# The last two tiles of self-attention and the entry into the feed-forward: another order on TensorE, and PSUM waits by tile

## The chip, the cores and the metric

The kernel runs on one core of a Trainium2 chip. The metric is the device time of one execution in microseconds (us); a time without other words is the median of the runs. The core has five engines with queues of their own: TensorE (PE in the profile; its weight loads are PEld), VectorE (DVE), ScalarE (ACT), GpSimd (POOL) and SyncE (SP), which issues most of the DMAs. [...]

## What is computed

One layer over x of 32 sequences x 64 tokens x 512: a cross-attention to a memory of 1601 tokens per sequence, a causal self-attention with 16 heads of 32, and a feed-forward of 2048 hidden units, each added to x. All in fp32. Cut to what matters here:

```python
x = x + xattn(layernorm(x), ctx, mask, ...)          # stage 1
Q, K, V = heads(n @ WQ), heads(n @ WK), heads(n @ WV)  # stage 2, n = layernorm(x)
score = softmax(Q @ K.T / sqrt(32) + causal)
x = x + (score @ V) @ WO
h = gelu(x' @ absmean(W_fc).T)                        # stage 3, x' = layernorm(x)
h = (h - mean(h)) * rsqrt(var(h) + 1e-5) * ln_w + ln_b
x = x + h @ absmean(W_proj).T
```

absmean turns a weight matrix into -1, 0 and 1. The layer norm of h is applied behind the last product: the kernel needs for it the sums of h and of h squared over the 2048 units, and two rows of 512 numbers that depend on the weights alone, `ln_w @ W_proj` and `ln_b @ W_proj`. These two rows are the "sides".

## The kernel before, in words

The 2048 tokens lie in 16 tiles of 128, which stay in SBUF (`xres`, tile i is `xs[i]`). After the cross-attention comes `self_attention` (L1201), which works tile by tile (i from 0 to 15, loop at L1394), and then `feed_forward` (L1440), which works in 4 groups of 4 tiles. A group has 16 hidden units, and a unit is 128 of the 2048 hidden rows for 512 tokens. One unit is `hidden` (L1166): 8 matmuls into a PSUM tile `fh` (L1172; four with the high and four with the low half of the input, `fxh` and `fxl`), then on ScalarE gelu into `bank` (L1180) and a square `fsq` (L1182), and two additions on VectorE into `sums` (L1188, L1189), which the caller runs later through the function that `hidden` returns.

Tile i of the self-attention takes these steps:

- `normalise(i, s)`: VectorE divides the exponentials by their sum (`atot`, L1331 to L1333).
- `turn(i, s)`: PE transposes the scores in two PSUM tiles `aptp` (L1343); ScalarE and VectorE copy them into `wo` by turns, 8 copies, each waiting for the one before (L1348).
- `mix(i)`: 32 small matmuls into `po` (L1356), copied by ScalarE into `aoT` (L1364).
- `exponentials(i + 1)`: the scores of the next tile (`sc`, L1304), VectorE's scaling, maximum and subtraction (L1309 to L1319), and ScalarE's exponential (L1326).
- `self_out(i, oT)`: 8 matmuls from aoT into `aout` (L1370); VectorE adds the result to xres (L1373).

Between them, `next(steps)` puts in three chunks of other PE work per tile. Up to tile 13 these are the projections for the next pair of tiles (`aWQ`, `aWK`, `aV`). For the last two tiles there are no more, so `first_hidden` (L1281) gives the first 12 hidden units of the feed-forward instead, two to a chunk: units 0 to 5 in tile 14 and 6 to 11 in tile 15. `add_up` (L1288) runs the additions that are still due.

The sides are made at the end of tile 14 (`sides`, L1133): 16 matmuls into 4 rows of a PSUM tile (L1136) and a copy by VectorE (L1139). In tile 15, between `mix` and `self_out`, `spread` (L1141) brings the rows to all partitions: for each of two, a product (L1144, four matmul records in all) and a ScalarE copy (L1145).

The order of the work: `in_order` (L145) chains all PE, VectorE, ScalarE and GpSimd instructions of `self_attention` to the order in which the code issues them, engine by engine, and does the same for those of `feed_forward`. Between the two lists nothing is chained, so an instruction of the second list may come before a late one of the first on the same engine. The page and the timeline show this: hTh and hTl, the halves of the first units for the products y (`split`, L1505, with L1517 on ScalarE and L1518 on VectorE), run before the residual addition of tile 15.

PSUM has eight banks. In `self_attention` the tag "mm" has three of them in turn (all of aptp, aout, sides, spread, fh), the scores sc have four and po has one. In `feed_forward` the units have two (`fs_m`), the transposes and statistics two (`fs_t`) and the four outputs y of a group four (`fs_y`). A pool opens in the place of pools that were closed. As the kernel is written, the first tile of each new pool waits until everything that used the old pools in that place is done.

The feed-forward's first PE work is unit 12 into `fs_m`, then the products y (L1523) of unit 0 for four tiles, then on with a unit and 8 product matmuls by turns.

Of the kernel before, what the change touches and what calls it, by code (L numbers as in the profile page):

```python
# [26 lines left out]
PSUM = bass.MemoryType.PSUM  # L27
# [4 lines left out]
NT = B * T // P  # L32
# [7 lines left out]
GT = 4  # L40
# [40 lines left out]
def perceiver_kernel(ctx: ExitStack, tc: tile.TileContext, a: dict, out: bass.AP):  # L81
# [63 lines left out]
    def in_order(begin, kinds=(Engine.PE, Engine.DVE, Engine.Activation, Engine.Pool)):  # L145

        before = {}
        for ins in nc.cur_bb.bb.instructions[begin:]:
            if ins.engine not in kinds or isinstance(ins, mybir.BassTileRelease):
                continue  # L150
            if ins.engine in before:
                tc.add_manual_dep(
                    ins,
                    before[ins.engine],
                    mybir.DependencyInfo(mybir.DependencyClass.NoSync, mybir.DependencyReason.DATA),
                    reason="in order",
                )
            before[ins.engine] = ins.name
# [104 lines left out]
    with ExitStack() as st:  # L263
# [10 lines left out]
        m8, table, steps = (opening[:, i:j] for i, j in zip(CUTS, CUTS[1:]))  # L274
        table = table[:B].bitcast(F32).rearrange("p (k b) -> p k b", b=B)
        steps = steps[:B].bitcast(F32).rearrange("p (k c) -> p k c", c=NC)
# [793 lines left out]
    def load_piece(pool, j, why):  # L1070
        r = pool.tile([P, D], F32, tag="raw", name=f"raw_{why}_{j}")
        put = nc.sync.dma_start(r, pieces[j])
        if why == "g":
            tc.keep_in_program_order(put)
        return r
# [20 lines left out]
    def compare(pool, j, w):  # L1096

        r, k = load_piece(pool, j, "q"), j // FC
        nc.vector.tensor_scalar(w, r, thr[:, 1, k : k + 1], None, ALU.is_lt)
        nc.vector.scalar_tensor_tensor(  # L1100
            w, r, thr[:, 0, k : k + 1], w.bitcast(F32), ALU.is_gt, ALU.subtract
        )
# [98 lines left out]
    def self_attention(st, wf, wp, first, ffn_input, ffn_turned, hidden, sides, measured):  # L1201

        raw = st.enter_context(tc.tile_pool(name="raw", bufs=2))
        p1 = st.enter_context(tc.tile_pool(name="a1", bufs=1))
        p2 = st.enter_context(tc.tile_pool(name="a2", bufs=2))
        ps_m = st.enter_context(tc.tile_pool(name="as_m", bufs=3, space=PSUM))
# [13 lines left out]
        def piece_of(j):  # L1220
            return wf[:, j // 4, j % 4 * D : (j % 4 + 1) * D] if j < FC else wp[:, j - FC, :]

        def group_spreads(g):
            return spreads([xs[g * GA + t] for t in range(GA)], 1e-5, f"a{g}")
# [12 lines left out]
        def heads(g, xT, order=range(6)):  # L1237


            QT = p2.tile([P, DC, GA * P], F32, tag="QT", name=f"QT_{g}")  # L1240
            KT = p2.tile([P, DC, GA * P], F32, tag="KT", name=f"KT_{g}")
            V = p2.tile([P, GA, D], F32, tag="V", name=f"V_{g}")
            made[g] = QT, KT, V

            def turned(w, dst, m0, copy):
                ps = ps_m.tile([P, 2, GA * P], F32, tag="mm", name=f"a{w}_{g}_{m0}")
                for m in range(2):
                    for c in range(DC):
                        nc.tensor.matmul(  # L1249
                            ps[:, m, :],  # L1250
                            ws[w][:, c, (m0 + m) * P : (m0 + m + 1) * P],
                            xT[:, c, :],
                            start=(c == 0),
                            stop=(c == DC - 1),
                        )
                copy(dst[:, m0 : m0 + 2, :], ps)

            def values(i):
                ps = ps_m.tile([P, D], F32, tag="mm", name=f"aV_{g}_{i}")
                for c in range(DC):  # L1260
                    nc.tensor.matmul(  # L1261
                        ps,
                        xT[:, c, i * P : (i + 1) * P],
                        ws["WV"][:, c, :],
                        start=(c == 0),
                        stop=(c == DC - 1),
                    )
                nc.scalar.copy(V[:, i, :], ps)

            for k in order:  # L1270
                if k % 3 == 0:
                    turned("WQ", QT, 2 * (k // 3), nc.scalar.copy)
                elif k % 3 == 1:
                    turned("WK", KT, 2 * (k // 3), nc.vector.tensor_copy)
                else:
                    values(k // 3)
                yield
# [3 lines left out]
        def first_hidden():  # L1281

            for n in range(12):
                adds.append(hidden(n, first, ps_m, "mm", raw, "raw"))
                if n % 2:
                    yield

        def add_up():  # L1288
            for add in adds:
                add()  # L1290
            adds.clear()
# [32 lines left out]
        def exponentials(i):  # L1324
            s = scores(i)
            nc.scalar.activation(s, s, AF.Exp)  # L1326
            return s

        def normalise(i, s):
            tot = small.tile([P, HEADS], F32, tag="atot", name=f"atot_{i}")  # L1330
            nc.vector.tensor_reduce(tot, s, AX.X, ALU.add)  # L1331
            nc.vector.reciprocal(tot, tot)
            nc.vector.tensor_tensor(  # L1333
                s, s, tot.unsqueeze(2).to_broadcast([P, HEADS, T]), ALU.mult
            )

        def turn(i, s):
            pairs = s.rearrange("p (j e) k -> p j (e k)", e=2)
            into = pT.rearrange("p (j e) q -> p j e q", e=2)
            for j in range(0, HEADS // 2, 4):  # L1340
                tp = ps_m.tile([P, 4, P], F32, tag="mm", name=f"aptp_{i}_{j}")
                for k in range(4):
                    nc.tensor.transpose(tp[:, k, :], pairs[:, j + k, :], ident)  # L1343
                for b in range(2):
                    half = slice(b * T, (b + 1) * T)
                    for e in range(2):
                        eng = nc.vector.tensor_copy if e else nc.scalar.copy
                        eng(into[half, j : j + 4, e, half], tp[e * T : (e + 1) * T, :, half])  # L1348
# [18 lines left out]
        def self_out(i, oT):  # L1367
            ps = ps_m.tile([P, D], F32, tag="mm", name=f"aout_{i}")
            for c in range(DC):
                nc.tensor.matmul(  # L1370
                    ps, oT[:, c, :], ws["WO"][:, c, :], start=(c == 0), stop=(c == DC - 1)
                )
            nc.vector.tensor_tensor(xs[i], ps, xs[i], ALU.add)  # L1373
# [20 lines left out]
        for i in range(NT):  # L1394
            g, t = divmod(i, GA)
            ahead = g + 2 < groups
            k = (i - 5) // 2
            begun = list(chores.get(i, ()))
            if t == 0:
                steps = heads(g + 1, xT) if g + 1 < groups else first_hidden()  # L1400
            next(steps)
            normalise(i, s)
            add_up()
            next(steps)
            turn(i, s)
            add_up()
            if t == 0:
                if 5 < i < 13:
                    xns = apply(fsp)
                if ahead:  # L1410
                    sp = group_spreads(g + 2)
            else:
                if ahead:
                    axns = apply(sp)
                if 4 < i < 12:
                    fsp = spreads([xs[k]], 1e-5, f"f{k}")
            for j in begun[1:]:
                compare(raw, j, piece_of(j))
            next(steps)
            if t == 0:  # L1420
                if 5 < i < 13:
                    ffn_turned(k, xns[0], first, ps_m, "mm")
            elif ahead:
                xT = turned_group(g + 2, axns)
            oT = mix(i)
            if i + 1 < NT:
                s = exponentials(i + 1)
            else:
                spread()
            add_up()  # L1430
            self_out(i, oT)
            for j in begun[:1]:
                compare(raw, j, piece_of(j))
            if i == NT - 2:
                side = p1.tile([P, DC, GA * P], F32, tag="xT", name="side")
                spread = sides(ps_m, "mm", side.rearrange("p c t -> p (c t)")[:, :D])
        in_order(begin)
        return 12

    def feed_forward(st, wp, lnw, Wwb, sums, first, slot, ffn_input, ffn_turned, hidden, done, store):  # L1440
        fx = st.enter_context(tc.tile_pool(name="fx", bufs=1))
        ft = st.enter_context(tc.tile_pool(name="ft", bufs=3))
        fq = st.enter_context(tc.tile_pool(name="fq", bufs=2))
        ps_m = st.enter_context(tc.tile_pool(name="fs_m", bufs=2, space=PSUM))
        ps_t = st.enter_context(tc.tile_pool(name="fs_t", bufs=2, space=PSUM))
        ps_y = st.enter_context(tc.tile_pool(name="fs_y", bufs=GT, space=PSUM))
        second = [fx.tile([P, DC, GT * P], F32R, name=f"fx{k}_1") for k in ("h", "l")]
        inputs = [first, second]
        G = NT // GT
# [263 lines left out]
```

## Time and profile before

| what | value |
|---|---|
| runs | 904.86, 904.89, 901.55 us; median 904.86 |
| the profiled execution | 902.01 us, of which the span from first to last instruction is 899.1 |
| granted TensorE clock, mean | 0.998 |
| cross-attention and start, 0 to 500 us | TensorE busy 493.08 us |
| self-attention, 500 to 613 us | TensorE busy 113.00 of 113.00 us |
| last tiles, 613 to 642 us | TensorE busy 28.07 of 29.00 us |
| last tile and entry, 642 to 662.4 us | TensorE busy 18.98 of 20.40 us |
| feed-forward, 662.4 to 893 us | TensorE busy 230.21 of 230.60 us |

In the lines of the profile `aout<-bank,aoT` reads: writes aout, reads bank and aoT; "128*128 128x512 f32 x8" is the size of the weights, the shape of the moving operand, its type and how many. A bracket such as `[0.73 <-ACT aoT L1364]` gives the idle time of the engine just before the instruction and the instruction whose end ended it. Durations of neighbouring matmuls overlap, since they are pipelined: what a group takes from the engine is read from the start of one to the start of the next.

### The profile page before, as it was taken

Reading aid. Unit: us, or ns where it says so; the run is one execution under the profiler, and the core shown is the slowest. Engines: PE = TensorE matmul, PEld = TensorE weight load, DVE = VectorE, ACT = ScalarE, POOL = GpSimd, SP = SyncE. Lnnn points to the kernel's source line nnn. Section 1 sums busy time; section 2 is a strip of 40 time slices with the busy share of each in tenths; the row PEclk is TensorE's granted clock in tenths of the full one; section 3 lists DMA queues with packets and bytes.
Section 4 is the critical chain, followed back from the end, with each engine's and each line's share of the span. In section 5 each row is a group of like instructions: output and inputs, shape, how many; then the busy total and the mean of one; then the engine's idle time right before and its main releaser. Section 6 shows DMA issues by size and latency. Waiting matters only on the chain.

```text
span 899.1 us, 12923 instructions
## 1 busy us (share of the span) xinstructions
PE 883.5 (98%) x4536; PEld 635.2 (71%) x4536; DVE 626.6 (70%) x1198; ACT 377.9 (42%) x811; POOL 67.3 (7%) x79
## 2 busy tenths in 40 slices
PE   9999999999999999999999999999999999999997
PEld 4456777777777767667666776676668878788885
DVE  5875656455655672588889888886776886876864
ACT  2554545545445431222232323224555555555550
POOL 0110111111101100000000000000001000010000
PEclk9999999999999999999999999999999999999999
DMA  8975898775585343011111010100000020010101
GB/s 269 320 248 181 235 243 248 233 248 156 181 252 171 109 132 129 1 59 36 48 36 48 24 36 24 36 12 1 1 1 1 1 47 1 6 42 1 31 17 52
DMA packets 58723, 88.05 MB, mean 98 GB/s; under 512 B 10516, under 2 KB 30872, under 8 KB 58264
## 3 DMA queue, kind: packets, MB, share of 16 engines
q1 hardware_dynamic: 57888, 86.58, 32.0%
q8 instruction: 38, 0.62, 0.3%
q10 hardware_dynamic: 760, 0.55, 0.2%
q14 instruction: 37, 0.30, 0.1%
HBM read 78.72 MB, written 4.19 MB: 92 GB/s over the span
## 4 chain that ended last, share of the span: by engine, by line
PE 86%; DVE 9%; ACT 3%; issue 1%; DMA 1%; POOL 0%; POOLq 0%; ACTq 0%
PE y L1523 13%; PE kvp L523 13%; PE fh L1172 11%; PE xo L645 6%; PE aV L1261 5%; PE aWQ L1249 5%; PE aWK L1249 5%; PE aout L1370 5%; PE q L231 5%; PE lgp L565 3%; PE enc L629 3%; PE sc L1304 1%; PE pt L614 1%; PE aptp L1343 1%; PE po L1356 1%; DVE s L1309 1%
## 5 line engine op out<-in xcount | busy, mean ns | idle before, releaser
L523 PE MATMUL kvp<-wkv,ct 128*128 128x256 f32 x576 | 134.7, 379 | 0.0
L523 PEld LDWEIGHTS kvp<-wkv,ct 128*128 128x128 f32 x576 | 107.0, 190 | 21.6 <-issue 8.8
L1523 PE MATMUL y<-wp,hTh 128*128 128x512 f32 x236 | 94.4, 400 | 0.4 <-DVE xres L1500 0.4
L1523 PE MATMUL y<-wp,hTl 128*128 128x512 f32 x236 | 92.8, 393 | 0.0
L1172 PE MATMUL fh<-fxh,wf 128*128 128x512 f32 x256 | 71.6, 401 | 1.3 <-DVE mv_f L128 0.9
L1180 ACT ACTIVATE bank<-fh 128x512 f32<-128x512 f32 x64 | 38.2, 597 | 77.0 <-PE fh L1172 76.9
L1172 PE MATMUL fh<-fxl,wf 128*128 128x512 f32 x256 | 70.4, 397 | 0.0
L530 ACT ACTIVATE kv<-kvp,rstd 128x256 f32<-128x256 f32 x72 | 34.0, 473 | 82.4 <-PE kvp L523 82.3
L572 DVE CUSTOM_DVE_ANT_0 pr<-lgp,bias 128x384 f32<-128x384 f32 (+6 forms) x64 | 28.5, 458 | 50.6 <-PE lgp L565 50.3
L1370 PE MATMUL aout<-bank,aoT 128*128 128x512 f32 x128 | 59.2, 605 | 1.1 <-ACT aoT L1364 1.1
L1518 DVE SCALAR_TENSOR_TENSOR hTl<-bank,lnw,hTh 128x512 fp32r<-128x512 f32 x59 | 44.0, 749 | 20.7 <-ACT hTh L1517 20.7
L645 PE MATMUL xo<-wo,encT 128*128 128x512 f32 x128 | 57.7, 594 | 0.2 <-ACT encT L638 0.2
L231 PE MATMUL q<-xres,wo 128*128 128x512 f32 x128 | 56.4, 593 | 0.6 <-DVE wo L346 0.6
L1172 PEld LDWEIGHTS fh<-fxl,wf 128*128 128x128 f32 x256 | 48.3, 189 | 11.2
L1172 PEld LDWEIGHTS fh<-fxh,wf 128*128 128x128 f32 x256 | 46.6, 188 | 13.2 <-issue 2.2
L1523 PEld LDWEIGHTS y<-wp,hTh 128*128 128x128 f32 x236 | 44.4, 188 | 14.0 <-DVE xres L1500 3.4
L1188 DVE TENSOR_TENSOR sums<-sums,bank 128x512 f32<-128x512 f32 x56 | 38.5, 687 | 20.8 <-ACT bank L1180 20.7
L1326 ACT ACTIVATE s<-s 128x1024 f32<-128x1024 f32 x15 | 15.9, 1059 | 86.5 <-DVE s L1319 86.5
L1523 PEld LDWEIGHTS y<-wp,hTl 128*128 128x128 f32 x236 | 44.5, 188 | 9.9
L1261 PE MATMUL aV<-bank,axT 128*128 128x512 f32 x112 | 51.2, 600 | 0.0
L1348 ACT COPY wo<-aptp 64x256 f32<-64x256 f32 x64 | 23.3, 365 | 66.2 <-PE aptp L1343 48.9
L1249 PEld LDWEIGHTS aWQ<-axT,bank 128*128 128x128 f32 x224 | 42.6, 190 | 11.8 <-issue 6.7
(176 smaller groups left out, 1562.0 us busy)
## 6 DMA issues: line engine op xcount, KB each, us to landing
nat<-in_ctx_dram SPq DMA_DIRECT2D x64, 256.0 KB, 5.0
ct<-in_ctxT_dram SPq DMA_DIRECT2D x7, 768.0 KB, 4.6
xres<-in_x_dram SPq DMA_DIRECT2D x8, 512.0 KB, 6.3
xres<-in_x_dram SPq DMA_DIRECT2D x32, 128.0 KB, 5.1
qs<-bank SPq DMA_DIRECT2D x32, 128.0 KB, 3.8
raw_g<-in_W_fcT_dram SPq DMA_DIRECT2D x16, 256.0 KB, 4.5
raw_g<-in_W_projT_dram SPq DMA_DIRECT2D x16, 256.0 KB, 3.5
raw_q<-in_W_fcT_dram SPq DMA_DIRECT2D x16, 256.0 KB, 2.9
```

Source lines behind the costliest of these rows:

```text
L231: nc.tensor.matmul(ps, wq[:, c, h, :], wide(g)[:, c], start=(c == 0), stop=(c == DC - 1))
L523: nc.tensor.matmul(ps.rearrange("p k h -> p (k h)"), cts[p][:, c, j * P : (j + 1) * P], wkv[:, c].rearrange("p k h -> p (k h)"), start=(c ...
L530: nc.scalar.activation(kvs[p][:, j], ps, AF.Copy, scale=rstds[p][:, j : j + 1])
L645: nc.tensor.matmul(o, encT[:, h].rearrange("p s t -> p (s t)"), wo[:, h, :], start=(h == 0), stop=(h == NH - 1),)
L1172: nc.tensor.matmul(ps, wf[:, c, cols], part[:, c, :], start=(i == 0 and c == 0), stop=(i == 1 and c == DC - 1),)
L1180: nc.scalar.activation(g, ps, AF.Gelu)
L1188: nc.vector.tensor_tensor(sums[:, 0], so_far[0], g, ALU.add)
L1249: nc.tensor.matmul(ps[:, m, :], ws[w][:, c, (m0 + m) * P : (m0 + m + 1) * P], xT[:, c, :], start=(c == 0), stop=(c == DC - 1),)
L1261: nc.tensor.matmul(ps, xT[:, c, i * P : (i + 1) * P], ws["WV"][:, c, :], start=(c == 0), stop=(c == DC - 1),)
L1370: nc.tensor.matmul(ps, oT[:, c, :], ws["WO"][:, c, :], start=(c == 0), stop=(c == DC - 1))
L1518: nc.vector.scalar_tensor_tensor(lo, g, w, hi.bitcast(F32), ALU.mult, ALU.subtract)
L1523: nc.tensor.matmul(y, part[:, t, :], wp[:, c, :], start=(c == 0 and i == 0), stop=(c == FC - 1 and i == 1),)
```

## The change

Three edits, none of which adds or removes a matmul, a copy or a DMA.

- The sides are made in tile 14 between the scores of tile 15 and `self_out(14)`, where they came after `self_out(14)`.
- `first_hidden` yields after units 1, 3, 5, 7, 8, 10 and 11, where it yielded after every second one. In tile 15 the three chunks are now units 6 and 7, unit 8, units 9 and 10, and a fourth `next(steps)` puts unit 11 between `spread` and `self_out(15)`. A second `add_up` after `self_out` runs its additions; in all other tiles it finds none.
- The three PSUM pools of `feed_forward` get `reuse_waits="tile"`: a tile of the new pool waits for those old tiles alone that lay in its own place.

```diff
@@ first_hidden
             for n in range(12):
                 adds.append(hidden(n, first, ps_m, "mm", raw, "raw"))
-                if n % 2:
+                if n in (1, 3, 5, 7, 8, 10, 11):
                     yield
@@ the loop over the tiles
             else:
                 spread()
             add_up()
-            self_out(i, oT)
-            for j in begun[:1]:
-                compare(raw, j, piece_of(j))
             if i == NT - 2:
                 side = p1.tile([P, DC, GA * P], F32, tag="xT", name="side")
                 spread = sides(ps_m, "mm", side.rearrange("p c t -> p (c t)")[:, :D])
+            if i == NT - 1:
+                next(steps)
+            self_out(i, oT)
+            add_up()
+            for j in begun[:1]:
+                compare(raw, j, piece_of(j))
@@ feed_forward
-        ps_m = st.enter_context(tc.tile_pool(name="fs_m", bufs=2, space=PSUM))
-        ps_t = st.enter_context(tc.tile_pool(name="fs_t", bufs=2, space=PSUM))
-        ps_y = st.enter_context(tc.tile_pool(name="fs_y", bufs=GT, space=PSUM))
+        ps_m = st.enter_context(tc.tile_pool(name="fs_m", bufs=2, space=PSUM, reuse_waits="tile"))
+        ps_t = st.enter_context(tc.tile_pool(name="fs_t", bufs=2, space=PSUM, reuse_waits="tile"))
+        ps_y = st.enter_context(tc.tile_pool(name="fs_y", bufs=GT, space=PSUM, reuse_waits="tile"))
```

## The prediction

> **What bounds the kernel now.** I read the page's busy shares first, then its chain of work that ended last, then TensorE's timeline around the change, and last the chain and VectorE's timeline there.
>
> ```profile
> PE 883.5 (98%) x4536; PEld 635.2 (71%) x4536; DVE 626.6 (70%) x1198; ACT 377.9 (42%) x811; POOL 67.3 (7%) x79
> ...
> PEclk9999999999999999999999999999999999999999
> ...
> PE 86%; DVE 9%; ACT 3%; issue 1%; DMA 1%; POOL 0%; POOLq 0%; ACTq 0%
> ```
>
> TensorE (PE) is busy for 98% of the span at the full granted clock and carries 86% of the chain. So only time in which TensorE stands still is to be had. The change keeps every matmul of before and reorders some, so its worth is the standstill that it closes. The timeline of TensorE from 630 to 665 us (start, duration, line, tiles, and in brackets the idle time before and who ended it) shows what there is:
>
> ```profile
> 632.68 1.17 PE L1304 MATMUL sc<-KT,QT 32*128 32x128 f32 x32
> 634.58 3.70 PE L1370 MATMUL aout<-bank,aoT 128*128 128x512 f32 x8 [0.73 <-ACT aoT L1364]
> 637.72 4.27 PE L1136 MATMUL sides<-wp,lnp 128*4 128x512 f32 x16
> ...
> 652.44 1.18 PE L1172 MATMUL fh<-fxh,wf 128*128 128x512 f32 x4 [0.21 <-DVE wo L1348]
> ...
> 655.48 1.98 PE L1144 MATMUL spread<-side,pick 4*128 4x512 f32 x4
> 657.80 3.70 PE L1370 MATMUL aout<-bank,aoT 128*128 128x512 f32 x8 [0.34 <-ACT aoT L1364]
> 662.37 1.17 PE L1172 MATMUL fh<-fxh,wf 128*128 128x512 f32 x4 [0.87 <-DVE mv_f L128]
> ```
>
> Three stalls lie where the edits are. Each output product `aout` (tiles 14 and 15) waits for ScalarE's copy aoT, 0.73 and 0.34 us, and the first hidden unit of the feed-forward (fh 12) waits 0.87 us for VectorE. The chain in order of time names the same three:
>
> ```profile
> 634.05 0.48 ACT aoT L1364
> 634.58 3.70 PE aout L1370 x8
> ...
> 657.27 0.48 ACT aoT L1364
> 657.80 3.71 PE aout L1370 x8
> 661.54 0.69 DVE xres L1373
> 662.23 0.10 DVE mv_f L128
> 662.37 2.10 PE fh L1172 x8
> ```
>
> fh 12 computes nothing from xres. It waits because its PSUM pool opens only when the pool before is free, and that pool's last reader is the residual addition of tile 15 (xres, L1373).
>
> **Part 1: sides ahead of aout in tile 14.** Nothing is added: the same 16 matmuls and one VectorE copy (0.68 us) move ahead of the same 8 matmuls and one addition (0.69). No DMA moves, and the POOL and SP queues have nothing in the stretch. After the scores of tile 15, PE takes `sides`, which needs neither aoT nor new data; its PSUM place was last read by the transposes' copies, over before 630.9. What the stall costs, by starts: scores to the next product is 1.90 us here (632.68 to 634.58) against 1.10 in tile 13 (614.28 to 615.38), so 0.80; by the bracket 0.73. aoT ends at 634.5, and aout would now start at 633.8 + 3.7 to 4.1 = 637.5 to 637.9, 3 us behind it. Saved: 0.73 to 0.80.
>
> What is late next? VectorE's list is now side copy, then addition of tile 14, which waits for an aout ending at 641.2 to 641.6. VectorE reaches it only at 641.98:
>
> ```profile
> 640.62 0.69 DVE L1189 TENSOR_TENSOR sums<-sums,fsq 128x512 f32<-128x512 f32 x1
> 641.33 0.69 DVE L1373 TENSOR_TENSOR xres<-aout,xres 128x512 f32<-128x512 f32 x1
> 642.02 0.68 DVE L1139 COPY side<-sides 4x512 f32<-4x512 f32 x1
> 642.63 1.20 DVE L1331 TENSOR_REDUCE atot<-s 128x16 f32<-128x1024 f32 x1
> ```
>
> The two lines L1373 and L1139 change places and the sum atot starts at the same 642.6. Queued behind the added wait is the whole softmax of tile 15, for which its transposes wait; the cover is 0.4 us.
>
> **Part 2: seven chunks for six in tile 15.** Units 6 to 11 (1.86 us each: fh starts at 641.82, 643.68, 645.54, 647.40) ran as two before the transposes' normaliser, two before the transposes and two behind. Now it is two, one, two, and unit 11 stands alone between the `spread` matmuls and aout of tile 15. There it covers aoT. Spread to aout takes 2.32 us now (655.48 to 657.80); its four matmuls start at 0.47 us intervals (655.5 to 656.9), 1.87 in all, so 0.45 is lost by starts, 0.34 by the bracket. With unit 11 in between, aout starts 1.9 us later than it could and aoT, which took until 0.05 before aout, is long there. Saved: 0.34 to 0.45.
>
> The price is cover taken from the transposes of tile 15. They would start at 649.26 - 0.80 - 1.86 = 646.6. The normalised scores s end at 645.4 (644.15 + 1.23), 1.2 us earlier. VectorE's additions of units 6 and 7 end at 647.8 and its first copy of the transposes is due 1.74 us (651.00 - 649.26) after they start, at 648.3: 0.5 us of cover. So nothing is charged, and the 0.21 us wait of the unit behind them stays. On ScalarE, fsq of the next unit no longer waits 1.25 us for the sum of unit 8 before it, since only one unit is waiting to be summed there.
>
> **Part 3: PSUM waits tile by tile.** All tiles with tag mm share three places in turn. Both versions make 21 of them in tiles 14 and 15, so aout of tile 15 keeps its place. In the built program of before this is bank 2, and fh 12 is in bank 0. Bank 0 would be left last by fh 11 (in before by spread 1). Its reader, gelu on ScalarE (0.60), is over some 3 us before aout ends. The four y tiles lie over the scores and po, read long before. So fh 12 follows aout of tile 15 at once. By starts: aout to fh 12 to y takes 6.51 us (657.80, 662.37, 664.31), and the same pair with no wait, aout of tile 13 to fh 0 to fh 1, 5.40 (615.38, 618.52, 620.78): 1.11, or 0.87 by the bracket. Behind fh 12 come the products y, which need the halves hTh and hTl of units 0 to 2. VectorE made these at 658.46 to 660.78, in its wait for aout of tile 15, which still exists. The only VectorE work put behind that wait is the sum of unit 11 (2 x 0.69).
>
> Does the new wait cost something? The nearest row is one semaphore instruction on PE's queue at L1144, 51 ns, hidden under po. [...] The bounds for it are 0 and 0.4 (8 such rows uncovered); 0 is nearer to the row.
>
> **Sum.** By brackets 0.73 + 0.34 + 0.87 = 1.94; by starts 0.80 + 0.45 + 1.11 = 2.36. I take 2.1 us, about the middle. From 662.4 to 893.0 PE is busy for 230.21 of 230.60 us, so what is won at the entry is kept to the end. The profiled execution took 902.01 us (span 899.1 and 2.9 around it) and would take 899.9. The runs shown are 904.86, 904.89 and 901.55, so it lies in the lower part. From the median 904.86 the forecast is **902.8 us**. A difference of 0.5%, about what a measurement of this kernel can tell from no change, is 4.5 us: this change can't reach it by its own stalls.
>
> **The rivals.**
> - *The entry still waits.* Either tile waits do nothing here (the change doesn't do what it says), or the entry's stall moves on: if VectorE does the residual addition and the sum of unit 11 (0.69 + 1.38) before hTl of unit 0 (0.74), then hTl is there 2.8 us after aout ends instead of before it, and y needs it 2.1 us after. 0.7 to 1.1 of the gain goes. For it: a list order decides this, which the profile of before doesn't show. Against: before, VectorE did these halves and even a BATCH_NORM_STATS2 (660.71) ahead of that addition. Gain 1.2 us: 903.7.
> - *Nothing gained.* Every stall is taken over by the next wait, the transposes' copies above all: 904.9.
> - *Slower: VectorE slips before the transposes of tile 15.* Place: the addition of tile 14, now behind a product that starts about 3.3 us later, with the softmax of tile 15 queued behind it. Each us of slip beyond the 0.5 us of cover stops PE at the transposes or the copies behind them. With a gain of 2.1 it decides from a slip of 2.6 us. If sides ran at its single matmul's 419 ns x 16 = 6.7 us and not the 4.1 between its starts, aout would end at 644.2 and the slip be 2.2; with a slip of one whole aout, 3.7, it costs 3.2 and the time is 906.0. Against: in before, sides and aout follow each other in 7.24 us from first start to fh (634.58 to 641.82), and the order of the two doesn't change that.
>
> **How the numbers follow.** Forecast 0.62 (902.8), entry still waits 0.22 (903.7), nothing gained 0.08 (904.9), slower 0.08 (906.0). The runs of before differ by 3.3 us with no change, so the median can land in the lower part: 901.55 - 2.4 = 899.1 is the lower end. The upper end is no gain, 904.9; only the slower case is left out. The forecast alone spans 899.1 to 902.9. Faster by over 0.5% (below 900.3) happens only where the forecast meets the lower run, 0.14; slower by over 0.5% (above 909.4) would take a slip of over 7 us, 0.04; the rest is 0.82.
>
> **What would show it.** In the profile after: sides follows the scores and aout of tile 14 has no bracket; fh stands between spread and the last aout, which has none either; fh 12 starts about 3.1 us after the last aout with no bracket; the first y stands at about 662.2 instead of 664.31 on the same time axis; the 0.21 us at the copies stays. Wrong would be: a bracket at aptp or a grown one behind it in tile 15 (VectorE slipped), one at the first y with DVE hTl (entry still waits), fh 12 with DVE as before (tile waits idle), or a time that moves by more than 3 us while these stalls move by 2, which would mean that something outside this stretch moved.

## The result, and the profile after

The changed kernel takes 901.46 us (median of 21 runs) against 903.35 of the kernel before (21 runs): the ratio is 0.9979, 95% interval 0.9972 to 0.9985, or 1.9 us less (1.4 to 2.5). The forecast was 2.1 us less. The profiled execution took 901.30 us, span 898.5. The number came true, but a part of its reasons did not. As an absolute time the forecast was 902.8 us, 1.3 us over the result: it started from the three runs known then, with a median of 904.86.

The timeline of TensorE after the change, over the same stretch as before:

```profile
633.37 1.17 PE L1304 MATMUL sc<-KT,QT 32*128 32x128 f32 x32
634.47 3.86 PE L1136 MATMUL sides<-wp,lnp 128*4 128x512 f32 x16
638.17 3.59 PE L1370 MATMUL aout<-bank,aoT 128*128 128x512 f32 x8
...
647.21 1.04 PE L1343 MATMUL aptp<-ident,s 128*128 128x128 f32 x8
...
650.38 1.16 PE L1172 MATMUL fh<-fxh,wf 128*128 128x512 f32 x4 [0.20 <-DVE wo L1348]
...
653.43 1.98 PE L1144 MATMUL spread<-side,pick 4*128 4x512 f32 x4
655.34 1.20 PE L1172 MATMUL fh<-fxh,wf 128*128 128x512 f32 x4
...
657.31 3.60 PE L1370 MATMUL aout<-bank,aoT 128*128 128x512 f32 x8
661.69 1.19 PE L1172 MATMUL fh<-fxh,wf 128*128 128x512 f32 x4 [0.78 <-DVE xres L1373]
...
663.66 0.39 PE L1526 MATMUL y<-wp,hTh 128*128 128x512 f32 x1
```

Both brackets at aout are gone. The one at fh 12 stayed: 0.78 us instead of 0.87, for the residual addition that the third edit was to make it independent of. From the start of sc of tile 15 to the first y it takes 30.29 us instead of 31.63, so the stretch gave 1.34 us. From the first y to the end of the span it is 234.84 us after 234.79: nothing is given back, and nothing gained there. This stretch, "sc to y", is the yardstick for all runs below, since it leaves out what lies ahead of it and wanders from one execution to the next: in fourteen profiles sc starts between 631.9 and 633.6 us. It is read from one execution of each kernel, though, and the one of before (902.01 us) is faster than the median of before.

VectorE's list in tiles 14 and 15 of the kernel after:

```profile
642.02 0.68 DVE L1139 COPY side<-sides 4x512 f32<-4x512 f32 x1
642.63 0.67 DVE L1373 TENSOR_TENSOR xres<-aout,xres 128x512 f32<-128x512 f32 x1
643.23 1.20 DVE L1331 TENSOR_REDUCE atot<-s 128x16 f32<-128x1024 f32 x1
...
648.95 0.43 DVE L1348 COPY wo<-aptp 64x256 f32<-64x256 f32 x1 [0.57 <-ACT wo L1348]
```

The sum atot starts 9.86 us after sc, 9.95 before: the softmax did not slip. VectorE reaches the residual addition at 642.63, 0.87 us after aout has ended (638.17 + 3.59), where the prediction had 0.4 us of cover. The bracket of 0.57 us ahead of the first copy is the cover that the prediction put at 0.5.

### The profile page after: what moved, and what is told of

It is laid out like the page before. It is cut to its first block, busy times and chain, and to the rows that moved or that the text cites. A ratio compares the mean times of both kernels' runs of the same rounds, so it can differ in the third digit from the quotient of the medians.

```text
span 898.5 us, 12926 instructions
## 1 busy us (share of the span) xinstructions
PE 883.5 (98%) x4536; PEld 635.4 (71%) x4536; DVE 627.1 (70%) x1198; ACT 377.8 (42%) x811; POOL 67.2 (7%) x79
## 4 chain that ended last, share of the span: by engine, by line
PE 87%; DVE 9%; ACT 2%; issue 1%; DMA 1%; POOL 0%; POOLq 0%; ACTq 0%
PE y L1526 13%; PE kvp L523 13%; PE fh L1172 12%; PE xo L645 6%; PE aV L1261 5%; PE aWQ L1249 5%; PE aWK L1249 5%; PE aout L1370 5%; PE q L231 5%; PE lgp L565 3%; PE enc L629 3%; PE sc L1304 2%; PE po L1356 1%; PE pt L614 1%; PE aptp L1343 1%; DVE s L1309 1%
```

## The experiments

Theory: each edit is worth the stall that it closes, and the third is worth nothing here because fh 12 lies in the PSUM bank of the last aout. The built programs say so: places of the tag mm are not handed out in turn, as the prediction took it. In the kernel before, fh 11, spread, spread and aout got the banks 2, 1, 0 and 2. In the changed one spread, spread, fh 11 and aout got 0, 2, 1 and 0. fh 12 is in bank 0 in both. Rivals: tile waits do nothing in any order, or VectorE's order holds the entry up.

| run | time, us | before, us | ratio, 95% interval | sc to y, us |
|---|---|---|---|---|
| before | | | | 31.63 |
| changed | 901.46 | 903.35 | 0.9979, 0.9972 to 0.9985 | 30.29 |
| E1 both orders, pool waits | 901.35 | 903.16 | 0.9983, 0.9973 to 0.9993 | 30.35 |
| E2 tile waits alone | 901.61 | 903.16 | 0.9981, 0.9971 to 0.9991 | 30.53 |
| E3 sides alone | 902.00 | 903.49 | 0.9984, 0.9975 to 0.9993 | 30.75 |
| E4 chunks alone | 901.67 | 903.49 | 0.9989, 0.9980 to 0.9998 | 31.25 |
| E5 changed, fh 12 in bank 2 | 900.84 | 903.16 | 0.9975, 0.9966 to 0.9985 | 30.78 |
| E6 changed, less cover | 899.25 | 903.49 | 0.9954, 0.9940 to 0.9968 | 29.46 |
| E7 as E5, pool waits | 900.84 | 903.16 | 0.9980, 0.9972 to 0.9989 | 30.34 |
| E8 changed, unit 11 ahead of spread | 901.31 | 903.26 | 0.9981, 0.9972 to 0.9989 | 32.18 |
| E9 changed, spread three times | 907.81 | 903.26 | 1.0044, 1.0029 to 1.0060 | 38.63 |
| E10 as E6, pool waits | 901.00 | 903.26 | 0.9980, 0.9971 to 0.9988 | 30.57 |
| E11 units on both sides of spread | 899.54 | 903.26 | 0.9960, 0.9947 to 0.9973 | 31.22 |
| E12 as E9, 128 rows | 903.43 | 903.49 | 1.0008, 0.9999 to 1.0017 | 33.52 |

**E1, the changed kernel without the third edit.**

```diff
-... name="fs_m", bufs=2, space=PSUM, reuse_waits="tile"))
+... name="fs_m", bufs=2, space=PSUM))       (fs_t and fs_y likewise)
```

> The changed kernel without its third edit: the two orders stay, the feed-forward pools wait as a whole again. In the built program the last aout and fh 12 lie in the same bank, 0. Theory (the place decides, so the third edit does nothing here): sc of tile 15 to the first y takes 30.3 us as in the changed kernel, give or take 0.15, the bracket at fh 12 stays 0.8 to 0.9, and the time is 1.3 to 1.9 us under before. Rival (tile waits are worth something elsewhere, in the first y tiles or the statistics): the stretch or the feed-forward grows by 0.3 us or more.

```profile
660.77 1.17 PE L1172 MATMUL fh<-fxh,wf 128*128 128x512 f32 x4 [0.88 <-DVE xres L1373]
```

Measured: 30.35 us, and fh 12 waits for the residual addition as in the changed kernel. The third edit does next to nothing there (0.06 us). Nor does it cost: from sc to the end, the changed kernel with its eight tiles that wait for themselves is not the slower one (265.1 us in both). The prediction's upper bound of 0.4 us for it, eight rows of 51 ns, was an estimate.

**E2, the kernel before with the third edit alone.** The diff is that of the change, its last part only.

> The kernel before with the third edit alone. In the built program aout of tile 15 lies in bank 2 and fh 12 in bank 0. Theory (place decides): fh 12 waits only for ScalarE's copy of spread, long done, so its bracket goes and the stretch from sc of tile 15 to the first y shrinks from 31.63 to 30.5 to 30.8 us; time 0.9 to 1.1 us under before. Rival (tile waits do nothing in this program, or VectorE's list moves the stall to the first y): stretch 31.4 us or more, time as before.

TensorE's timeline of E2:

```profile
656.43 1.98 PE L1144 MATMUL spread<-side,pick 4*128 4x512 f32 x4
658.76 3.70 PE L1370 MATMUL aout<-bank,aoT 128*128 128x512 f32 x8 [0.34 <-ACT aoT L1364]
661.89 1.49 PE L1172 MATMUL fh<-fxh,wf 128*128 128x512 f32 x4
```

fh 12 follows aout after 3.13 us, with no bracket, where the kernel before takes 4.57. The stretch is 1.10 us shorter. So the edit works in the order of before, where the two tiles lie in different banks, and the second edit, by its order, brought them into one: in the built programs the last aout is in bank 2 with the first edit alone (E3) and in bank 0 with the second alone (E4).

**E3 and E4, the first and the second edit alone**, each in the kernel before.

> The kernel before with the first edit alone (sides ahead of aout in tile 14). Theory: the 0.73 us bracket at aout of tile 14 goes, the two others stay (0.34 and 0.87), sc of tile 15 to the first y goes from 31.63 to 30.8 to 30.9 us, and the time falls by 0.7 to 0.8 us. Rival (VectorE slips, since the residual addition of tile 14 waits for a later product ahead of the softmax): the sum atot of tile 15 starts over 0.5 us later after sc than before (9.95 us), and the stretch stays at 31.4 or more.

> The kernel before with the second edit alone (two, one, two units and unit 11 behind spread). Theory: the bracket at the last aout (0.34) goes, the ones at aout of tile 14 (0.73) and fh 12 (0.8 to 0.9) stay, stretch 31.1 to 31.3 us, time 0.3 to 0.5 us under before. Rival (the transposes of tile 15 lose their cover): a bracket at the transposes or a longer one behind them, stretch 31.6 or more.

Measured: 0.88 us (31.63 - 30.75) and 0.38 us (31.63 - 31.25). atot starts 9.86 us after sc in E3, so VectorE doesn't slip, and E4 has no bracket at the transposes. The three edits alone sum to 0.88 + 0.38 + 1.10 = 2.36 us, which is the prediction's sum by starts to the hundredth (the single terms are off by up to 0.08); together they give 1.34.

**E5 and E7, the changed kernel with `fs_t` opened ahead of `fs_m`**, with tile waits and with pool waits.

```diff
-        ps_m = st.enter_context(... "fs_m" ...)
         ps_t = st.enter_context(... "fs_t" ...)
+        ps_m = st.enter_context(... "fs_m" ...)
```

> The changed kernel with the first two feed-forward pools opened in the other order, so that fh 12 lies in bank 2, whose last content is spread, and the first transposes in bank 0. Theory (place decides): fh 12 follows the last aout with no bracket, sc of tile 15 to the first y takes 29.1 to 29.4 us (30.3 less 0.9 to 1.1), and the time is 2.2 to 3.0 us under before. Rival (the stall moves to the first y, since hTl and the sum of unit 11 stand behind it on VectorE): fh 12 without bracket, but y with one of 0.7 us or more, and the time as the changed kernel.

> As the run with the pools opened in the other order, but with waits for whole pools. Theory: the place alone is worth nothing without tile waits, fh 12 waits for the residual addition, stretch 30.3 us and time as the changed kernel, 0.9 to 1.1 us over the run with tile waits. Rival (what helps is the other place, not the wait): no bracket, stretch 29.1 to 29.4 us.

In E5 fh 12 has no bracket, 3.18 us after aout, and the first y none either. In E7 it has 0.88. So the wait and the place are needed together, and the sum of unit 11 on VectorE holds nothing up. But E5's stretch was 30.78 and not 29.1 to 29.4, and by their times the two cannot be told apart (both 900.84 us), where 0.9 to 1.1 was expected. Its table by stretches (length, then busy time and count of PE, PEld, DVE, ACT and POOL, then the granted clock, DMA share and GB/s) shows why:

```profile
653.00:655.00 2.00, 2.00 (x13) 0.68 (x5) 2.00 (x5) 2.00 (x5) 0.00 (x0) 1.00 0.00 0
655.00:657.00 2.00, 2.00 (x6) 1.62 (x6) 1.60 (x3) 1.73 (x4) 0.00 (x0) 0.56 0.04 8
657.00:659.00 2.00, 2.00 (x6) 1.39 (x5) 1.45 (x4) 0.39 (x1) 0.34 (x1) 0.58 0.00 0
659.00:661.00 2.00, 2.00 (x6) 0.90 (x5) 0.00 (x0) 0.84 (x2) 0.20 (x1) 1.00 0.00 0
```

TensorE was busy without a gap, and the clock granted to it fell to a half for 3.4 us, behind po and spread. Unit 11 took 3.38 us from its start to that of aout instead of the 1.97 of the changed kernel. The fall is no part of any theory so far; E8, E9 and E12 take it up. The mean clock of this execution is 0.998, like that of all 12 runs of E5, so the mean of a whole run does not always show such a fall.

**E6 and E10, one unit less ahead of the transposes**, with tile waits and with pool waits.

```diff
-                if n in (1, 3, 5, 7, 8, 10, 11):
+                if n in (1, 3, 5, 6, 7, 9, 11):
```

> The changed kernel with one unit less ahead of the transposes of tile 15: one, one, two units, and two (10 and 11) behind spread. It tests the cover I put at 0.5 us on VectorE and 1.2 us on the normalised scores. The transposes would start 1.87 us earlier than in the changed kernel, where VectorE waits 0.57 us for its first copy. Theory (cover is real and small): PE stops at the transposes or the unit behind them for about 1.87 - 0.57 = 1.3 us, or 0.7 us where the scores alone bind. Here the last aout and fh 12 lie in different banks, so 0.9 to 1.1 us come back at the entry; the stretch is 30.3 + 1.0 - 1.0, about 30.3, with the bracket moved from fh 12 to the transposes. Rival (VectorE has room): no new bracket, stretch 29.2 us and 2.2 to 3.0 us under before.

> The run with one unit less ahead of the transposes, but with waits for whole pools. There the last aout lies in bank 1 and fh 12 in bank 0. Theory (tile waits are worth 0.9 to 1.1 us where the places differ): the bracket of 0.87 at fh 12 comes back, stretch 29.46 + 1.0 = 30.4 to 30.6 us, and 1.0 us over that run. Rival (its gain comes from the chunks alone): stretch 29.5, no bracket.

TensorE's timeline of E6:

```profile
645.40 1.09 PE L1343 MATMUL aptp<-ident,s 128*128 128x128 f32 x8 [0.53 <-DVE s L1333]
...
656.89 3.60 PE L1370 MATMUL aout<-bank,aoT 128*128 128x512 f32 x8
659.93 1.48 PE L1172 MATMUL fh<-fxh,wf 128*128 128x512 f32 x4
```

The cover is gone and the transposes wait 0.53 us for the normalised scores. I had expected 0.7 to 1.3; VectorE's additions don't bind, since only one unit is due for summing there, and the 0.20 us wait behind the transposes is gone as well. In return aout and fh 12 lie in the banks 1 and 0, and the entry is free: 29.46 us, where about 30.3 was expected. E10 puts the wait back and 1.11 us with it (30.57):

```profile
661.47 1.17 PE L1172 MATMUL fh<-fxh,wf 128*128 128x512 f32 x4 [0.88 <-DVE xres L1373]
```

Tile waits are worth 1.1 us in both pairs of runs that differ in nothing else and hold the full clock (before and E2, 1.10; E10 and E6, 1.11). E6 is also the best version that was run: 899.25 us against 903.49 (5 runs), and under the changed kernel's ratio with its whole interval. Its time fell by 4.2 us (2.9 to 5.4), twice the 2.17 of its stretch. That is the prediction's last sign of being wrong, a time that moves by more than 3 us while the stalls move by 2. Its profile has the same 234.80 us from the first y on, so the rest is not explained.

**E8, unit 11 ahead of spread.**

```diff
+                next(steps)
                 spread()
...
-            if i == NT - 1:
-                next(steps)
             self_out(i, oT)
```

> The changed kernel with unit 11 ahead of spread and not behind it. Open is why the kernels are timed about 0.5 us further under before than their profiles' stretches say. Theory (clock): one profile so far has a stretch of 3.4 us at half the granted clock, from 655.3 us on, right behind po and spread, small matmuls (32 columns, 4 rows) that fill about 3 us in a row; in before 26 of 56 runs show a mean clock of 0.996 or 0.997 and take 1.2 to 1.4 us more, with unit 11 in place 11 of 73. With unit 11 between po and spread the small matmuls come in two pieces of 1.0 and 1.9 us, so hardly any run should show a clock under 0.998, at a stretch of 30.3 us as in the changed kernel. Rival (the low clock has nothing to do with this place): a share like that of before, 4 in 10 or more.

```profile
655.93 5.40 PE L1370 MATMUL aout<-bank,aoT 128*128 128x512 f32 x8
662.11 1.19 PE L1172 MATMUL fh<-fxh,wf 128*128 128x512 f32 x4 [0.78 <-DVE xres L1373]
```

The expectation fell. The profile has the half clock itself, from 656.3 to 659.7 us; without it (aout to fh 12 takes 6.18 us, 4.38 in the changed kernel) the stretch would be 30.4, about the expected 30.3. Parting po from spread by one unit doesn't prevent it. Spread alone, 1.9 us, seems enough. How often it comes is less clear: five of 11 runs show a mean clock of 0.997 or less, but only the two at 0.995, the profiled one among them, take longer (902.35 and 902.93 us). The three at 0.997 take 901.31 to 901.51, no more than the runs at 0.998 and 0.999.

**E9, spread three times, and E12, the same with 128 rows.**

```diff
-                    nc.tensor.matmul(ps, pick[:, k, :], side[:4], start=True, stop=True)
+                    for _ in range(3):
+                        nc.tensor.matmul(ps, pick[:, k, :], side[:4], start=True, stop=True)
...
E12: pick and side have 128 rows, zeros below the first four
-                        nc.tensor.matmul(ps, pick[:, k, :], side[:4], start=True, stop=True)
+                        nc.tensor.matmul(ps, pick[:, k, :], side, start=True, stop=True)
```

> The changed kernel with each spread product issued three times, which lengthens the stretch of small matmuls (po and spread) from 2.9 to 6.7 us; the repeats compute the same again. [...] Rival (small matmuls don't lower the clock): only the 3.8 us, 1.9 us over before, and the clock as in the changed kernel.

> The run with each spread product issued three times, but with 128 rows in place of 4: the other 124 rows of both operands are zeros, so that the result is the same. Theory (few rows lower the clock): no stretch at half the clock behind spread, runs at 0.998 or more, and only the 3.8 us of work over the changed kernel, 905.2 us or 1.9 us over before. Rival (the clock goes by something else, the many passes of fp32 or operands that are mostly zero): half the clock from 654 to 664 us as in the run with 4 rows, and 907 to 909 us.

E9 by stretches, then E12:

```profile
652.00:654.00 2.00, 2.00 (x16) 0.90 (x9) 2.00 (x4) 2.00 (x4) 0.00 (x0) 1.00 0.04 8
654.00:656.00 2.00, 2.00 (x4) 0.81 (x3) 2.00 (x4) 1.37 (x3) 0.00 (x0) 0.63 0.00 0
656.00:658.00 2.00, 2.00 (x4) 0.78 (x3) 1.04 (x4) 0.15 (x1) 0.54 (x1) 0.50 0.00 0
...
664.00:666.00 2.00, 2.00 (x5) 0.97 (x5) 0.00 (x0) 1.23 (x2) 0.00 (x0) 0.81 0.00 0
```

```profile
654.00:656.00 2.00, 2.00 (x6) 0.81 (x6) 2.00 (x4) 1.26 (x3) 0.00 (x0) 1.00 0.00 0
656.00:658.00 2.00, 2.00 (x8) 1.15 (x7) 0.79 (x3) 0.54 (x1) 0.54 (x1) 1.00 0.00 0
```

With 4 rows TensorE is busy and at half clock for some 10 us in the profile, and the time is 4.0 us over before (2.6 to 5.4), where 2.5 to 3.7 was expected. Not every execution has it: five of the 8 runs, the profiled one among them, have a mean clock of 0.993 to 0.995 and take 907.2 to 909.8 us, the other three 0.997 and 905.1 to 905.3. These three are 3.6 to 3.9 us over the changed kernel, about what the added work takes by itself.

With 128 rows, the same number of matmuls and the same result, the clock stays at 1.00 there, and the 11 runs lie between 902.6 and 904.0 us without such a group. Two of them, the profiled one included, have a mean clock of 0.997 where 0.998 was expected, though the profile shows no fall up to 896 us: the mean takes in the end of the run as well, where the clock is 0.72 from 896 to 897 us. The time is that of before (0.1 under to 1.5 over), less than the 1.9 over it that I expected. The 3.8 us of work were too much: I had counted 0.48 us per record (1.91 for four in the changed kernel), but within a group the records from the second on start 0.43 us apart, with 4 rows at full clock and with 128 alike, so that eight more are 3.4 us. So here it is the few rows in use that lower the clock (0.50 with 4 in E9, 1.00 with 128 in E12), not fp32 and not zeros, which E12 has as well. It is 0.50 for 3.4 us in the profiles of E5, E8 and E11; what sets this length is not shown. E9 has no gap there (2.00 of 2.00 us busy in each line above), and from 652.3 to 660.6 us only matmuls that use 4 of 128 rows.

**E11, the version that the runs pointed to**: unit 10 ahead of spread and unit 11 behind it, tile waits.

```diff
-                if n in (1, 3, 5, 7, 8, 10, 11):
+                if n in (1, 3, 5, 6, 7, 9, 10, 11):
...
+                next(steps)
                 spread()
```

> The version that the runs point to: one, one and two units in tile 15, unit 10 ahead of spread and unit 11 behind it, tile waits, the last aout in bank 1 and fh 12 in bank 0. Theory: the one stall of 0.53 us at the transposes stays, no bracket at either aout or at fh 12, stretch 29.4 to 29.6 us, all runs at a clock of 0.998 or more, 2.2 us under before by the stretch and up to 0.6 more by the clock. Rival: no better than the changed kernel, stretch 30.3.

899.54 us (5 runs): better than the kernel before, and not told apart from E6; against the changed kernel the two intervals just meet. Brackets as expected: 0.53 at the transposes, none at aout and fh 12. Its profiled execution met the half clock behind spread (655.6 to 659 us), hence 31.22 us and not 29.5: the expectation that the clock would stay up failed here too. That execution took 901.62 us at a mean clock of 0.998, the four others 899.3 to 900.2 at 0.999 or 1.0.

## Why the prediction was right, and where it was not

- **What bounds the kernel**: right. Only TensorE's standstill counted; all that was saved between sc and y was there at the end (234.8 us from y on, before and after).
- **Sides first**: right, 0.88 us by E3 where 0.73 to 0.80 stood. The check of what comes late next held: VectorE had cover, 0.87 us where 0.4 stood, and the softmax didn't move.
- **The chunk of one unit**: right, 0.38 us by E4 within 0.34 to 0.45. The cover at the transposes was 0.57 us against 0.5; E6 shows that the stall behind it is real.
- **Tile waits**: this step failed. It said that both versions make 21 tiles of the tag mm, "so aout of tile 15 keeps its place". It did not: by the order of the second edit it got bank 0, fh 12's own, and the prediction's own sign of being wrong came up, fh 12 with DVE as before. The term is 0.06 us (E1 to the changed kernel) in place of 0.87 to 1.11. Its size was right where the places differ: 1.10 in E2, 1.11 from E10 to E6. The 0.4 us that bounded the cost of the waits themselves is shown by no run: with them and without, sc to the end takes 265.1 us (changed kernel, E1). The same belief in turns put the sides over the transposes in tile 14; in the built program they lie over unit 4, in bank 2, which did no harm.
- **The rivals**: the stretch did what the first rival said ("tile waits do nothing here", gain 1.2 us; measured 1.34), though by a cause that it didn't name. The slower one never began: no slip on VectorE.
- **The total**: 2.1 us was forecast for three stalls, two of them went for 1.34 us, and 1.9 us (1.4 to 2.5) was measured. That the time fell within reach of the forecast is partly luck, since the 0.5 us between stretch and time was not in any term. The gap appears in E1, E2, E3, E4, E7 and E10 too: their stretches are 1.28, 1.10, 0.88, 0.38, 1.29 and 1.06 us shorter and their intervals centre on 1.5, 1.7, 1.4, 1.0, 1.8 and 1.8. In E6 it is 2.0 us. Part of it may lie in the one profile of before, an execution of 902.01 us where the median is 903.35. The clock may be the rest: of the 96 runs of before that were made beside the experiments, 49 have a mean clock of 0.997 or less and take 1.2 to 2.2 us longer than the others by the medians, and 3 of 21 of the changed kernel do, by 1.5 us. Against it stand three things. E2 and E3 both leave the order around spread as it was, and have 2 and 5 of 11 such runs. A mean of 0.997 is found in E12 without the half clock, and 0.998 in E5 with it. And no profile of before caught the half clock at work. Whether the changed order makes it rarer, and whether that is the 0.5 us, is not settled.

## What to carry to other kernels

A wait for a tile's own place was worth something here only where the place differed from that of the tile in the way (1.10 and 1.11 us, against 0.06); read the places in the built program after every change of order, since another order of the tiles can bring the two together (here bank 2 became 0). Price a stall by the starts of the work on its two sides against the same pair elsewhere in the trace: here the starts gave 2.36 us, the brackets 1.94, and the edits alone 2.36. When single stalls of under 1 us are closed, compare the stretch in the profile and not only the time, which here also holds the clock.

## What the runs showed of the hardware

TensorE can be busy without a gap and still lose its clock. Behind matmuls with 4 rows the granted clock was 0.50 for 3.4 us in the profiles of E5, E8 and E11 and for some 10 us in E9, and each such fall of 3.4 us lengthened the stretch by 1.5 to 1.9 us (E5 against E7 less 1.1; E8 against the changed kernel; E11 against E6). It comes in some executions of a kernel and not in others: five of the 8 runs of E9 are long, and the profile of the changed kernel, with the same matmuls around spread as E5, has none. With zeros in the other 124 rows the clock was 1.00 (E12). At full clock the two kinds of matmul followed each other alike, 0.43 to 0.44 us from start to start (weight loads of spread in the changed kernel at 653.96 and 654.39 us; E12's twelve matmuls start between 652.0 and 656.8 us). The `sides`, which use all rows and 4 columns for 3.7 us, showed no such fall in any profile: the clock was 1.00 from 633 to 642 us in all fourteen.
